# Sequence 1's tokens transposed on VectorE from rows folded in DRAM, two output copies issued two leaves later, and wf's first sums on GpSimd

## The chip, the cores and the metric

The kernel runs on one core of a Trainium2 chip. The metric is the device time of one execution in microseconds (us), as the median of several runs. The profile names the engines PE (TensorE, matmuls), PEld (its weight loads), DVE (VectorE), ACT (ScalarE), POOL (GpSimd) and SP (SyncE, which here only issues DMAs). Each engine takes its own instructions strictly in the order in which they stand in its queue; an instruction that waits for a semaphore holds up everything behind it on that engine, DMA issues included.

## The reference

Four sequences of 512 tokens, 512 features, in float32. One layer: a gated linear scan, then a feed-forward part with a Hadamard transform, each between layer norms and with a residual.

```python
x = x + layernorm(attn(layernorm(x)))
x = x + layernorm(ffn(layernorm(x)))

def attn(h):                       # Wi, Wf, Wg, Wo: 512 x 512
    i, f, g = h @ Wi.T, h @ Wf.T, h @ Wg.T
    gate = sigmoid(f);  v = silu(i) * (1 - gate)
    o_t = gate_t * o_(t-1) + v_t            # scan over the tokens
    o = o * rsqrt(mean(o * o) + eps) * gnorm_w * g * sigmoid(g)
    return o @ Wo.T

def ffn(h):                        # W1, W3: 2048 x 512, W2: 512 x 2048
    return fwht(silu(h @ W1.T) * (h @ W3.T)) @ W2.T
```

## The kernel before

**Products in seven pieces.** Every large matrix product is done by a seven-product scheme on 2x2 blocks (Strassen-Winograd). `ORDER` gives the products as P1, P2, P6, P5, P7, P3, P4; each reads one block or sum of blocks of the weights (A11 to A22, S1, S2, S3, S4) and one of the tokens (B11 to B22, T1 to T4). `combine_left` makes S1 and S2 (step 0) and S3 and S4 (step 1); `combine_right` makes T1 to T4. P1 and P2 read raw blocks alone; P6, the third, needs S2 and T2. The three PSUM banks of a product are X (P1, P6, P7, P4), Y (P2) and Z (P5, P3). A bank gathers: P4, say, is added into the bank that P7 left, so it waits until P7's value has been read out. P1, P6, P5 and P4 are read out by a copy on ACT, P2, P7 and P3 by an addition on DVE (L537).

**Units.** `attn_unit(b, u)` does one piece of the scan part of sequence b: u = 0 and u = 1 are the two halves of Wi and Wf (and end in the gate and the scan), u = 2 is Wg. The order begins with units (0,0), (0,1), (0,2), (1,0), (1,1). `run` walks through the seven products of a unit. After product k it takes what `beside[k]` lists, and, after every product if the unit is `dense`, else after products 1, 3, 5 and 6, one entry of the list `fill` (other work for PE: output products, the quarters of the Hadamard transform of W2). `seven` also takes entries of `acts` and `sums` at fixed products: activations and DVE or POOL work that belongs to earlier products.

**Order on the engines.** PE and SP have the order in which the code is written. The others are scheduled when the kernel is built; `behind(what)` puts work behind a named earlier instruction, and `tc.high_priority` moves it forward. What results is a fixed order for each engine.

**Layer norm and transposing.** `normalize_tiles(b, "a", i0, n)` takes statistics of a token tile (128 tokens) on DVE (`st_a`, L289; `mv_a`, L290), the inverse root as a power on POOL (`rs_a`, L264), the bias on DVE (`nb_a`, L303), and applies both on ACT (`xn_a`, L318). For sequence 0 the four tiles are done one by one as x arrives. The normalized tokens must be transposed, and there are two ways:

- `transposes(b, name)`: on PE against the identity, two groups of eight (`pt_a`, L439), copied from PSUM to `xt_a` by DVE and ACT (L446, L444), then `combine_right`. Sequences listed in `ON_TENSOR` go this way: 0 and 1.
- for the others, `normalize_tiles` writes the normalized tiles to DRAM in two DMAs from POOL's queue (`xnd_a`, L327, 512 KB each), `load_fold` reads them back folded (`fold_a`; from SP, with the 32-row blocks of four feature groups beside each other on the partitions), and `transpose_fold` transposes 32x32 blocks on DVE (L497), eight instructions, and then calls `combine_right`.

**Weights.** Raw weights of sequence 0's units come from the inputs (`wi`, `wf`, `wg`; two DMAs of 256 KB each, L199) and are combined on DVE; with S1 to S4 beside them they are 896 KB and are written to DRAM by POOL's queue (`s_wi`, `s_wf`, `s_wg`, L179). Later sequences load that from SP (L186). The `stream` pool has five buffers, so a load also waits until an earlier unit has let one go. The first unit's S1 and S2 are made by `combine_weights(2, (0,))`, S3 and S4 later.

**The end of sequences 0 and 1.** `OutputNorm.half_onto` normalizes the feed-forward output `f` (POOL root, ACT L412) and adds it to the residual rows, kept in DRAM, by an accumulating DMA from POOL's queue (`s_x<-f`, L416); the next DMA on the same queue copies those rows to the output (`out_dram<-s_x`, L417), and waits for the first. POOL also has work of the running products in its queue there (`q`, L946, part of the outer combination in `ffn_pair`).

Of the kernel before, what the change touches and what calls it, by code (L numbers as in the profile page):

```python
# [44 lines left out]
def kernel(  # L45
# [14 lines left out]
    nc = tc.nc  # L60
# [5 lines left out]
    NJ = NF // 2  # L66
# [3 lines left out]
    URGENT, SOON = 400, 200  # L70
# [23 lines left out]
    fill = deque()  # L94
# [7 lines left out]
    beside = {}  # L102
# [52 lines left out]
    def combine_left(t, eng, steps=(0, 1)):  # L155

        if 0 in steps:
            eng.tensor_add(t[:, S1], t[:, A21], t[:, A22])  # L158
            eng.tensor_sub(t[:, S2], t[:, S1], t[:, A11])
        if 1 not in steps:  # L160
            return
        eng.tensor_sub(t[:, S3], t[:, A11], t[:, A21])
        return eng.tensor_sub(t[:, S4], t[:, A12], t[:, S2])  # L163
# [41 lines left out]

    uncombined = []

    def combine_weights(n=None, steps=(0, 1)):
        for _ in range(len(uncombined) if n is None else n):
            key, t = uncombined.pop(0)  # L210
            read["combined"] = combine_left(t, nc.vector, steps)
            if 1 in steps:
                kept(key, t)
            else:
                uncombined.append((key, t))
# [3 lines left out]
    def load_attn_w(b, u):  # L219
        if u < 2:  # L220
            attn_w[b, u] = weight(wi, "wi", u, b), weight(wf, "wf", u, b)
        else:
            attn_w[b, u] = weight(wg, "wg", 0, b), weight(wg, "wg", 1, b)
# [26 lines left out]
    def behind(what):  # L250


        return tc.issue_after(read[what].ins)
# [12 lines left out]

    xns, xnd = {}, {}

    ON_TENSOR = ("a", 0), ("a", 1)

    def normalize_tiles(b, name, i0, n, later=False):

# [78 lines left out]
    class OutputNorm:  # L351
# [47 lines left out]
        def half_onto(self, i, rows, to):  # L399

            b, mv = self.b, self.mv[:, 2 * i : 2 * i + 2]
            name = f"{self.name}_{b}_{i}"
            for t in range(2):
                nc.vector.bn_aggr(mv[:, t, :], self.st[:, 2 * i + t])
            r = inverse_root(mv, self.eps, name)
            nm = small.tile([P, 2], F32, tag="nb", name=f"nm_{name}", bufs=8)
            nc.vector.tensor_scalar(nm, mv[:, :, 0], -1.0, None, ALU.mult)
            nc.gpsimd.tensor_mul(nm, nm, r)

            def piece(t):  # L410
                y_t = self.y[:, i, t, :]
                nc.scalar.activation(  # L412
                    y_t, y_t, AF.Identity, bias=nm[:, t : t + 1], scale=r[:, t : t + 1]
                )
                if t:
                    nc.gpsimd.dma_start(out=rows, in_=self.y[:, i], accum_op=ALU.add)  # L416
                    nc.gpsimd.dma_start(out=to, in_=rows)  # L417

            scaled.extend([1, partial(piece, t)] for t in range(2))

# [700 lines left out]
    def load_w2(pieces):  # L1121
        for j in pieces:
            if j in (4, 5):
                t = stream2.tile([P, 3, D], F32, tag="w", name=f"w2p_{j}")
            else:
                t = work.tile([P, 3, D], F32, tag="ht", name=f"w2p_{j}", bufs=4)
            if j >= HALVES:
                for b, r in enumerate((chunks(j).start, chunks(j).start + 2)):
                    nc.sync.dma_start(
                        out=t[ts(b, P // 2), 0:2, :], in_=w2_quarters[:, r, :, :]  # L1130
                    )
            else:
                rows = w2_rows[:, chunks(j), :]
                for k in ((0, 1), (1, 2)) if j == 0 else ((0, 2),):
                    nc.sync.dma_start(
                        out=t[:, k[0] : k[1], :], in_=rows[:, k[0] : k[1], :]
                    )
            w2_p.append(t)
# [140 lines left out]
    later = uncombined[2:]  # L1279
    del uncombined[2:]  # L1280
    with behind("xt"):
        combine_weights(2, (0,))
    with behind("power"):
        load_constants()

# [12 lines left out]
        butterfly_b(0)  # L1298
    for k, j in ((0, 2), (1, 3)):
        low_step(k, "P2", butterfly_u, j)  # L1300
    fill.extend([None] + quarters[:2])
    attn_unit(0, 1)
    with behind("P3"):
        with tc.high_priority(offset=URGENT):
            combine_weights(2)
        with tc.high_priority(offset=SOON):
            apply = [normalize_tiles(1, "a", i, 2, True) for i in (0, 2)]
    load_attn_w(1, 0)
    load_w2(range(4, NJ))

    def behind_copy(*makes):
        with behind("copy"):
            for make in makes:
                make()

    fill.extend(
        [None, partial(behind_copy, *apply)] + transposes(1, "a")
    )
    for k, c in ((0, 0), (2, 1)):
        beside.setdefault(k, []).append(  # L1320
            partial(behind_copy, partial(scale_wo, wo_t[0], c))
        )
    attn_unit(0, 2)
    load_attn_w(1, 1)
    load_x(2)

    def beside_copies(b, places):
# [2 lines left out]
            late = [normalize_tiles(b, "a", i, 2, True) for i in (0, 2)]  # L1330
        for t, place in enumerate(places):
            yield place, partial(behind_copy, partial(late[t // 2], range(t % 2, t % 2 + 1)))

    def transpose_beside(b, name, places=((1, "P2"), (4, "P7"), (6, "P3"))):


        def step(make, what):
            with behind(what), tc.high_priority(offset=SOON):
                make()

        for make, (k, what) in zip(transpose_fold(b, name), places):
            beside.setdefault(k, []).append(partial(step, make, what))

    fill.extend([None] * 3 + attn_out(0) + quarters[-4:])
    for k, what, make, at in (
# [291 lines left out]
```

## Time and profile before

| | |
|---|---|
| median of 3 runs | 783.71 us (783.34 to 784.11) |
| profiled execution, its own time | 784.42 us |
| span of the profile | 782.6 us |
| PE busy | 764.2 us (98%) |
| DVE, ACT, POOL busy | 615.7, 240.0, 357.2 us |
| unit (0,0): P1, P6, P4 start | 11.32, 17.14, 24.72 us |
| units (0,1), (0,2), (1,0), (1,1) start | 26.55, 41.07, 55.06, 74.58 us |

Start times are from the timeline of PE, counted from the start of the span; 1.8 us of the execution lie outside the span. The granted TensorE clock is 1.00 in every stretch of 10 us up to 770. In the profile's lines a group reads: start, duration, engine, line, operation, output<-inputs, shapes, count, and in brackets the idle time ahead of it and what ended that. SPq and POOLq stand for the instructions that an engine issues without being counted as busy.

### The profile page before, as it was taken

What the parts mean: (1) busy time and instruction counts of PE and PEld (TensorE: products, weight loads), DVE (VectorE), ACT (ScalarE), POOL (GpSimd) and SP (SyncE); (2) the same over time, 40 slices, a digit from 0 to 9 for tenths busy, and PEclk for the clock granted to TensorE, in tenths of its full rate; (3) what the DMA queues carried; (4) which work ended last, traced back from release to release, by engine and by line L of the source; (5) the groups of instructions that cost most, each with busy time, mean ns of one, the idle gap of its engine ahead of it and who ended that gap; (6) DMA issues with size and microseconds to landing.
All of it is one profiled execution on the core that took longest, in us unless ns stands there. A gap on an engine that the chain in (4) does not pass through costs nothing.

```text
span 782.6 us, 10415 instructions
## 1 busy us (share of the span) xinstructions
PE 764.2 (98%) x3560; PEld 658.0 (84%) x3560; DVE 615.7 (79%) x1158; ACT 240.0 (31%) x337; POOL 357.2 (46%) x444
## 2 busy tenths in 40 slices
PE   8999999999999999999999999999999999999994
PEld 6788788887888888888888888888888888888883
DVE  5879989799877597898689799998645666664786
ACT  4383664545436232424112111021321100111112
POOL 1111202213302001177596968677767756664372
PEclk9999999999999999999999999999999999999998
DMA  9998474896899899983429420442456141121112
GB/s 267 394 339 313 155 263 168 253 342 227 295 368 336 269 295 397 361 269 99 157 80 217 149 78 9 150 99 70 99 173 159 52 151 55 54 75 74 54 55 107
DMA packets 90516, 147.29 MB, mean 188 GB/s; under 512 B 15136, under 2 KB 68512, under 8 KB 90208
## 3 DMA queue, kind: packets, MB, share of 16 engines
q1 hardware_dynamic: 79376, 94.98, 39.5%
q0 software_dynamic: 10368, 50.34, 17.6%
q10 hardware_dynamic: 720, 1.31, 0.5%
q8 instruction: 28, 0.46, 0.3%
q14 instruction: 24, 0.20, 0.1%
HBM read 97.32 MB, written 51.38 MB: 190 GB/s over the span
## 4 chain that ended last, share of the span: by engine, by line
PE 85%; DVE 7%; DMA 3%; POOL 2%; issue 2%; ACT 0%; SPq 0%; POOLq 0%; DVEq 0%; ACTq 0%
PE X_u L1042 18%; PE X_po L743 13%; PE X_a L562 9%; PE Z_u L1042 9%; PE Z_po L743 7%; PE X_f L562 5%; PE Z_a L562 4%; PE Y_u L1042 4%; PE Y_po L743 3%; PE X_y L670 3%; PE Y_a L562 2%; PE Z_f L562 2%; DMA wf<-in_Wf_dram 2%; PE Z_y L670 2%; POOL q L946 1%
## 5 line engine op out<-in xcount | busy, mean ns | idle before, releaser
L743 PE MATMUL X_po<-w,ht 128*128 128x256 f32 x512 | 139.1, 379 | 0.0
L1055 DVE TENSOR_TENSOR q<-X_u,q 128x512 f32<-128x512 f32 x132 | 90.5, 685 | 47.2 <-PE X_u L1042 42.7
L1042 PE MATMUL X_u<-xq,wl 128*128 128x256 f32 x480 | 123.3, 381 | 0.0
L743 PEld LDWEIGHTS X_po<-w,ht 128*128 128x128 f32 x512 | 97.3, 190 | 13.2
L1042 PEld LDWEIGHTS X_u<-xq,wl 128*128 128x128 f32 x480 | 90.5, 190 | 14.8 <-DVE q L1055 1.7
L987 ACT ACTIVATE q<-q 128x1024 f32<-128x1024 f32 x24 | 25.4, 1058 | 163.1 <-DVE q L1055 86.8
L946 POOL TENSOR_TENSOR q<-q,q 128x512 f32<-128x512 f32 x48 | 62.7, 1322 | 22.7 <-DVE q L1055 21.3
L743 PE MATMUL Z_po<-w,ht 128*128 128x256 f32 x256 | 69.1, 379 | 1.2 <-ACT f L539 1.2
L1055 DVE TENSOR_TENSOR q<-Z_u,q 128x512 f32<-128x512 f32 x72 | 49.4, 686 | 18.5 <-PE Z_u L1042 18.2
L562 PE MATMUL X_f<-xt_f,w 128*128 128x256 f32 x256 | 60.4, 381 | 1.9 <-DVE d_f L537 1.5
L1042 PE MATMUL Z_u<-xq,wl 128*128 128x256 f32 x240 | 61.6, 379 | 0.0
L179 POOL DMA_DIRECT2D s_w<-w x24 | 13.1, 545 | 99.9 <-DVE w L163 70.3
L562 PEld LDWEIGHTS X_f<-xt_f,w 128*128 128x128 f32 x256 | 48.2, 190 | 9.6 <-DVE d_f L537 2.3
L1052 ACT COPY q<-X_u 128x512 f32<-128x512 f32 x36 | 21.0, 585 | 114.6 <-PE X_u L1042 114.6
L743 PEld LDWEIGHTS Z_po<-w,ht 128*128 128x128 f32 x256 | 48.6, 190 | 8.2 <-ACT f L539 1.6
L1042 PEld LDWEIGHTS Z_u<-xq,wl 128*128 128x128 f32 x240 | 45.6, 190 | 6.2
L1042 PE MATMUL X_u<-og,wl 128*128 128x256 f32 x192 | 49.6, 381 | 1.1 <-DVE q L1055 1.1
L1055 DVE TENSOR_TENSOR q<-Y_u,q 128x512 f32<-128x512 f32 x42 | 28.8, 686 | 24.0 <-PE Y_u L1042 19.5
L158 POOL TENSOR_TENSOR ht<-ht 128x256 f32<-128x256 f32 x24 | 20.2, 843 | 59.8 <-DVE ht L999 59.8
L537 DVE TENSOR_TENSOR f<-X_po,f 128x512 f32<-128x512 f32 x51 | 34.8, 683 | 15.3 <-PE X_po L743 14.4
L1042 PEld LDWEIGHTS X_u<-og,wl 128*128 128x128 f32 x192 | 36.1, 190 | 7.2 <-issue 1.2
L999 DVE TENSOR_TENSOR ht<-q 128x512 f32<-128x512 f32 x48 | 41.3, 874 | 0.0
(230 smaller groups left out, 1589.6 us busy)
## 6 DMA issues: line engine op xcount, KB each, us to landing
s_w<-w POOLq DMA_DIRECT2D x24, 896.0 KB, 5.9
wl<-s_w SPq DMA_DIRECT2D x168, 128.0 KB, 2.5
w<-s_w SPq DMA_DIRECT2D x22, 896.0 KB, 7.8
w<-in_W_dram SPq DMA_DIRECT2D x32, 256.0 KB, 6.8
wi<-s_wi SPq DMA_DIRECT2D x6, 896.0 KB, 9.3
wf<-s_wf SPq DMA_DIRECT2D x6, 896.0 KB, 8.1
wg<-s_wg SPq DMA_DIRECT2D x6, 896.0 KB, 6.3
w_h<-w2p POOLq DMA_DIRECT2D x8, 512.0 KB, 5.5
```

What stands on the lines that cost most here:

```text
L158: eng.tensor_add(t[:, S1], t[:, A21], t[:, A22])
L179: return nc.gpsimd.dma_start(out=saved[key], in_=t)
L537: read[what] = nc.vector.tensor_add(to, ps[which], to)
L562: nc.tensor.matmul(ps[:, n, :], w[:, a, c, :], xt[:, bb, c, :], start=first and n == 0 and c == 0, stop=c == 1, skip_group_check=True,)
L670: nc.tensor.matmul(ps[:, t, :], og[:, a, c, ts(t, P)], w[c][:, bb, :], start=first and t == 0 and c == 0, stop=c == 1, skip_group_check=True,)
L743: nc.tensor.matmul(ps[:, t, :], hts[b, m][:, a, ts(t, P)], w[m][:, W2[bb], :], start=first and k == 0, stop=m == ms[-1], skip_group_check= ...
L946: queued.append(make(*args).ins)
L987: nc.scalar.activation(q[k][:, 0], q[k][:, 0], AF.Silu)
L999: nc.vector.tensor_mul(t[:, h : h + 3 : 2], d[:, 0, n].rearrange("p (t f) -> p t f", t=2), d[:, 1, n].rearrange("p (t f) -> p t f", t=2),)
L1042: nc.tensor.matmul(ps[which][:, k, :], w[:, k, a, :], x[:, bb, :], start=first and k == 0, stop=True, skip_group_check=True,)
L1052: read["copy"] = nc.scalar.copy(y, ps[which])
L1055: last = nc.vector.tensor_add(y, ps[which], z)
```

## The change

1. `ON_TENSOR` holds sequence 0 alone. Sequence 1 goes the way of sequences 2 and 3: its statistics are placed behind P2 of unit (0,0), its four tiles are applied on ACT beside products 0 to 3 of unit (0,1), they are written to DRAM (2 x 512 KB), and `load_fold(1, "a")` reads them back in four DMAs of 256 KB. That call stands ahead of `load_attn_w(1, 0)`, so on SP's queue the four loads stand behind the loads of wo and ahead of wi and wf of sequence 1, of the eight loads of W2's other quarters, and of what follows. The DVE transposes are placed beside products 4, 5 and 6 of unit (0,2).
2. Unit (0,1) becomes dense, and `fill` gets entries of None so that the two quarters stand at the same products as before. In PE's queue the sixteen transposes of sequence 1 are gone, and nothing else moves.
3. S1 and S2 of the first wf tile are made on POOL, not DVE. In the order that results, POOL has: the roots of tiles 0, 1 and 2 of sequence 0, the two sums of wf, the root of tile 3, then the rest. DVE keeps the two sums of wi, now behind the bias of tile 3.
4. In `half_onto`, the copy to the output is no longer issued right behind the accumulating DMA but goes to the list `sums` behind two empty entries. In POOL's queue this changes one place: two additions of `q` stand between the last accumulating DMA and the first of the two copies, and one between the copies.

The rest of the order of DVE and ACT shifts by a few places up to unit (1,1). The core of the diff:

```diff
-    def combine_weights(n=None, steps=(0, 1)):
+    def combine_weights(n=None, steps=(0, 1), eng=None):
...
-            read["combined"] = combine_left(t, nc.vector, steps)
+            read["combined"] = combine_left(t, eng or nc.vector, steps)
...
-    ON_TENSOR = ("a", 0), ("a", 1)
+    ON_TENSOR = (("a", 0),)
...
                     nc.gpsimd.dma_start(out=rows, in_=self.y[:, i], accum_op=ALU.add)
-                    nc.gpsimd.dma_start(out=to, in_=rows)
+                    copy = partial(nc.gpsimd.dma_start, out=to, in_=rows)
+                    sums.extend([lambda: None, lambda: None, copy])
...
     with behind("xt"):
-        combine_weights(2, (0,))
+        combine_weights(1, (0,))
+        combine_weights(1, (0,), nc.gpsimd)
...
-    fill.extend([None] + quarters[:2])
-    attn_unit(0, 1)
-    with behind("P3"):
-        with tc.high_priority(offset=URGENT):
-            combine_weights(2)
-        with tc.high_priority(offset=SOON):
-            apply = [normalize_tiles(1, "a", i, 2, True) for i in (0, 2)]
-    load_attn_w(1, 0)
-    load_w2(range(4, NJ))
+    fill.extend([None] * 3 + quarters[:1] + [None] + quarters[1:2])
...
-    fill.extend(
-        [None, partial(behind_copy, *apply)] + transposes(1, "a")
-    )
+    with behind("P2"):
+        apply = [normalize_tiles(1, "a", i, 2, True) for i in (0, 2)]
+    for k, t in ((0, 0), (1, 1), (2, 2), (3, 3)):
+        beside.setdefault(k, []).append(
+            partial(behind_copy, partial(apply[t // 2], range(t % 2, t % 2 + 1)))
+        )
+    attn_unit(0, 1, True)
+    with behind("P3"):
+        with tc.high_priority(offset=URGENT):
+            combine_weights(2)
+    load_fold(1, "a")
+    load_attn_w(1, 0)
+    load_w2(range(4, NJ))
...
+    transpose_beside(1, "a", ((4, "P7"), (5, "P3"), (6, "P3")))
     attn_unit(0, 2)
```

`transpose_beside` is the helper that sequences 2 and 3 already use; its definition only moves up.

## The prediction

> **What bounds the kernel now.** I read the page's totals first, then the chain that ended last in order of time, then the timelines of single engines around the three edits. Every time is microseconds from the start of the span.
>
> ```profile
> span 782.6 us, 10415 instructions
> PE 764.2 (98%) x3560; PEld 658.0 (84%) x3560; DVE 615.7 (79%) x1158; ACT 240.0 (31%) x337; POOL 357.2 (46%) x444
> ```
>
> PE is busy for 98% of the span, so PE work that goes is gained only if PE does not wait for something new. The chain's first pieces:
>
> ```profile
> 6.22 7.68 DMA wf<-in_Wf_dram
> 13.92 7.68 DMA wf<-in_Wf_dram
> 24.72 3.72 PE X_a L562 x16
> ```
>
> The second half of wf lands at 13.90; from 24.72 on the chain is nearly all PE. What happens around 13.90 (timelines of POOL, DVE, ACT and PE; a bracket is the idle time ahead and its cause):
>
> ```profile
> 10.26 0.55 POOL L264 TENSOR_TENSOR rs_a<-rs_a,power 128x1 f32<-128x1 f32 x1 [1.28 <-DVE rs_a L261]
> 13.93 0.43 DVE L158 TENSOR_TENSOR wf<-wf 128x256 f32<-128x256 f32 x1 [2.21 <-DMA wf<-in_Wf_dram]
> 11.40 0.84 ACT L318 ACTIVATE xn_a<-x,nb_a,rs_a 128x512 f32<-128x512 f32 x1
> 14.16 0.65 ACT L444 COPY xt_a<-pt_a 128x256 f32<-128x256 f32 x2
> 13.25 1.11 PE L439 MATMUL pt_a<-ident,xn_a 128*128 128x128 f32 x8
> 17.14 1.13 PE L562 MATMUL X_a<-xt_a,wi 128*128 128x256 f32 x4 [1.05 <-DVE xt_a L169]
> ```
>
> The root of token tile 3 (L264) is done at 10.81, long before wf; the tile is normalized at 11.40, transposed at 13.25; P6 of the first unit starts at 17.14, after waiting 1.05 for T2. The transposes that the change removes, and PE's neighbours there:
>
> ```profile
> 51.43 1.11 PE L439 MATMUL pt_a<-ident,xn_a 128*128 128x128 f32 x8
> 52.38 1.89 PE L562 MATMUL X_a<-xt_a,wg 128*128 128x256 f32 x8
> 54.11 1.11 PE L439 MATMUL pt_a<-ident,xn_a 128*128 128x128 f32 x8
> 55.06 1.03 PE L562 MATMUL X_a<-xt_a,wi 128*128 128x256 f32 x4
> ```
>
> PE runs through here without a gap. Sequence 1's first unit starts at 55.06, its wf products at 55.92. Last, what the same fold loads cost where the kernel has them already (SP's queue; then KB each and median us to landing):
>
> ```profile
> 206.26 2.12 SPq L472 DMA_DIRECT2D fold_a<-xnd_a  x4
> 209.81 0.55 SPq L186 DMA_DIRECT2D wf<-s_wf  x1
> wf<-s_wf SPq DMA_DIRECT2D x1, 896.0 KB, 15.0
> 259.27 2.15 SPq L472 DMA_DIRECT2D fold_f<-xnd_f  x4
> 261.51 1.09 SPq L186 DMA_DIRECT2D w<-s_w  x2
> w<-s_w SPq DMA_DIRECT2D x2, 896.0 KB, 8.9
> ```
>
> From the first fold load to the landing of the second 896 KB weight behind it: 209.81 + 15.0 - 206.26 = 18.5 where POOL's queue wrote two 896 KB weights at the same time (209.20, 210.20), and about 262.1 + 8.9 - 259.27 = 11.7 where it did not.
>
> **Part 1, wf's first sums on POOL.** In the instruction order POOL now has: roots of tiles 0, 1 and 2, the two sums of wf, root of tile 3. POOL takes its queue in order, and the sums wait for the wf half that lands at 13.90. So tile 3's root, done at 10.81 before, waits: two sums of 0.84 (the page's row of POOL's 128x256 adds, 843 ns; the wl adds of that shape take 0.73) to 15.6, root 0.55 to 16.2, bias on DVE 0.16 to 16.4, tile normalized on ACT 0.81 to 17.2. Behind that instruction stand on ACT two w2p copies (1.10), P1's copy (0.57) and two xt copies (0.65): 19.5. DVE waits at the bias with wi's sums behind it (two, 0.34 apart; ready by 17.1), then T1 and T2, 0.68 each and 0.1 between: about 20.6 instead of 17.1. P6 starts 3.5 later. P5, P7 and P3 follow at 1.73 each; before, PE had 0.6 of waiting ahead of 24.72, because DVE stood at the next wf (landing 21.60) with P7's addition behind it; that slack goes. Cost: +2.9. The lower end has PE alone late: transposes done at about 18.1, P2 until 19.9, so 2.7 - 0.6 = +2.1. Below that it goes only if tile 3's root is not held; then this term is nothing, since the wf landing at 21.60 still sets 24.72.
>
> **Part 2, transposes.** PE loses two groups of eight; each takes 0.95 from its start to the next instruction's (51.43 to 52.38, 54.11 to 55.06): -1.9. The rest of PE's order is unchanged, the quarters' matmuls included. DVE loses six copies of about 0.35 and gains eight transposes of 0.33 (four took 1.33 at 152.20): +0.6 on DVE, paid while PE waits for weights.
>
> The Trainium skill's VectorE: DVE Perf Modes, Rules for kernel authors, says to transpose 128x128 on TensorE where a PSUM destination is acceptable, which speaks against this change; this trace's price for keeping it there is the 1.9 of PE.
>
> The new way is a chain: statistics on DVE, root on POOL, four normalized tiles on ACT, two POOL writes of 512 KB to DRAM, four SP loads of 256 KB, transposes. Its place: DVE resumes unit 0 with P7's addition at about 26.4. To the second bias stand about fifteen instructions at a pitch of 0.60 (w2p butterflies, products' additions), four statistics at 0.57, two of 1.14 and 0.7 of small ones: 14.3, so 40.7 less about 0.4 for what is spread behind it: 40.3. Two tiles on ACT at 0.8: 41.9; the second write is issued at 42.0 and lands 3.7 later (median of xnd_a around 88): 45.7. Only then may SP issue the fold.
>
> Behind the fold on SP stand wi and wf of sequence 1 (issued at 33.98 and 40.40 before), eight w2p loads, the next wi and wf, and x of sequence 2. So wf lands between 45.7 + 11.7 = 57.4 and 45.7 + 18.5 = 64.2. POOL's two s_wg writes (896 KB each) are issued at about 45 to 46 here, beside the fold, as in the longer row, but without that row's extra 512 KB write and with a small head start. I take 14.9, a little under the middle of 15.1: 60.6. PE would be at its wf products at 55.92 + 2.9 - 1.9 = 56.9: a wait of +3.7 (ends +0.5 and +7.3). The fold itself lands 8 to 10 after its issue by the rows at 206 to 216, by 55.7; transposes, T1, og and T2 take 5.1 more, 60.8, before P6 needs T2 at about 63.
>
> ACT's new tiles stand ahead of P5's copy in unit (0, 1), which then ends about 0.7 before P3 needs its bank, and DVE's P7 addition ends 0.4 before P4. I cost both at nothing: what PE would lose is taken out of the wait for wf, which is longer. Without that wait, each miss is up to 1. The later SP loads (3.9 MB to the next wf) need 10 at the 390 GB/s of windows 20 to 50, and the s_wo writes 4.7: 75.5, against 74.58 + 4.7 = 79.3 when unit (1, 1) starts. Covered.
>
> The Trainium skill's TensorE: Matmul & The Clock Gate, Part 1, says that PE's clock halves after an idle window of about 3.4 us. Here the granted clock falls to 0.50 about 5 us after the last matmul (772.3 to 777.3), and no gap before is that long. The new gaps of about 3.7 are near that rule; one cold window would add an estimated 1.7, which I leave out by the trace's 5.
>
> **Part 3, output copies later.** POOL stood still for its accumulating write:
>
> ```profile
> 592.15 0.74 POOL L417 DMA_DIRECT2D out_dram<-s_x  x1 [3.65 <-DMA s_x<-f]
> 603.99 0.70 PE L743 MATMUL Z_po<-w,ht 128*128 128x256 f32 x2 [1.23 <-ACT f L539]
> ```
>
> Behind it stood q additions; ACT's gate waited for the last of them, the copy of Z_po for the gate, PE for the copy. With two additions ahead of the copy POOL is done about 3.6 earlier, and PE's gap goes: 603.99 instead of 602.16 + 0.43, -1.4. If the additions wait for DVE anyway, it is 0. In the order this is the only place where POOL's instructions change.
>
> **Sum.** Against the profiled execution (784.42: span 782.6 and 1.8 around it): +2.9 - 1.9 + 3.7 - 1.4 = +3.3, 787.7. The median of the runs is 783.71, 0.7 lower: 787.0.
>
> **Rivals.** (1) Weights in time: SP's queue is idle while it waits, so nothing else is loading, and the 11.7 row holds. The wait is 0.5, the sum +0.1: 783.8, no change. For it: the emptied load queue; against it: the s_wg writes. (2) The other end, 18.5: wait 7.3, sum +6.9: 790.6. (3) Faster: tile 3's root is not held on POOL. Then part 1 is 0, and the whole chain to the fold, which hangs on P7, moves up by the same 2.9. With the weights at the 11.7 row the sum is -1.9 + 0.5 - 1.4 = -2.8: 780.9 (with 14.9 it would be +0.4). It decides at the landing of wf: if that comes before about 10.3, when the root's input is ready, the sums cost the root little. Against it stands 13.90 in this trace, with the same loads ahead of it. (4) The copies' move does nothing: 1.4 more than each case.
>
> **How the numbers follow.** The forecast, slower, has 0.55; the longer end 0.12; no change (with the low edge of the forecast) 0.18; faster 0.15. A difference under 0.2% (1.6 us) can't be told from none here. So slower 0.67, same 0.18, faster 0.15. The range of 782.6 to 790.5 leaves out about 0.1 on each side: below lies most of the faster case, above half of the longer end.
>
> **What would show it.** On POOL two wf additions at 13.9 and tile 3's root after 15.5; P6 of unit (0, 0) near 20.6. No L439 group after 20. SP's fold near 46 and wi after it; in sequence 1's first unit a PE wait for wi or wf of 2 to 5, its start near 59. No gap on PE near 603. I am wrong if PE enters sequence 1 before 55, or if the root of tile 3 stays near 10.3.

## The result, and the profile after

The changed kernel takes 792.63 us (median of 4 runs, 789.72 to 795.74) against 783.76 (783.34 to 784.11) for the kernel before on the same chip. The ratio of the means is 1.0114, 95% interval 1.0067 to 1.0161: slower, by more than the forecast (787.0) and beyond the range's upper end (790.5). The profiled execution took 790.59; before's took 784.42, so the two traces differ by +6.17, and those 6.17 can be followed through the trace.

The page's totals after:

```profile
span 788.8 us, 10385 instructions
PE 765.8 (97%) x3544; PEld 658.6 (83%) x3544; DVE 617.6 (78%) x1158; ACT 241.6 (31%) x335; POOL 360.1 (46%) x448
```

PE has 16 instructions fewer, as the change says, and yet 1.6 us more busy time. The same matmuls took longer, so part of the loss is not waiting but clock: two windows of 3.41, told of below, ran at a granted clock of 0.50. Each keeps PE busy for about 1.7 longer; against the two stand the transposes' 1.9, which are gone.

**The start, timelines of POOL, ACT and PE** (line numbers are those of the changed kernel, which lie one higher from L417 on):

```profile
12.64 0.73 POOL L158 TENSOR_TENSOR wf<-wf 128x256 f32<-128x256 f32 x1 [3.82 <-DMA wf<-in_Wf_dram]
14.12 0.55 POOL L264 TENSOR_TENSOR rs_a<-rs_a,power 128x1 f32<-128x1 f32 x1
14.90 0.81 ACT L318 ACTIVATE xn_a<-x,nb_a,rs_a 128x512 f32<-128x512 f32 x1 [3.53 <-DVE nb_a L303]
15.77 1.03 PE L440 MATMUL pt_a<-ident,xn_a 128*128 128x128 f32 x4 [2.59 <-ACT xn_a L318]
16.59 1.92 PE L563 MATMUL Y_a<-xt_a,wi 128*128 128x256 f32 x4
19.75 1.03 PE L563 MATMUL X_a<-xt_a,wi 128*128 128x256 f32 x4
```

POOL waits 3.82 for wf, and tile 3's root comes out of it at 14.67 instead of 10.81: it is held, as the prediction said. The tile is normalized at 14.90 instead of 11.40, and PE stands 2.59 ahead of the last four transposes. Behind that gap the granted clock is 0.50 from 16.06 to 19.47, and P2's two groups take 3.16 (16.59 to 19.75), where before they took 1.73. When PE enters unit (0,1) it is 1.83 late (28.38 against 26.55).

**Unit (0,1), timelines of PE, PEld and DVE after, then the lines of before that answer to them:**

```profile
34.43 1.03 PE L563 MATMUL Z_a<-xt_a,wf 128*128 128x256 f32 x4
38.17 2.62 PE L1161 MATMUL h<-w2p,had 64*64 64x512 f32 x8 [2.72 <-DVE w2p L1151]
40.72 2.07 PE L563 MATMUL X_a<-xt_a,wi 128*128 128x256 f32 x4
39.35 0.20 PEld L1161 LDWEIGHTS h<-w2p,had 64*64 64x64 f32 x6 [1.02 <-DVE w2p L1152]
37.36 0.66 DVE L1151 TENSOR_TENSOR w2p<-w2p 128x512 f32<-128x512 f32 x1
38.61 0.69 DVE L1152 TENSOR_TENSOR w2p<-w2p 128x512 f32<-128x512 f32 x1
```

```profile
33.55 1.09 PE L1160 MATMUL h<-w2p,had 64*64 64x512 f32 x8
25.25 0.68 DVE L1150 TENSOR_TENSOR w2p<-w2p 128x512 f32<-128x512 f32 x1
27.05 0.68 DVE L1151 TENSOR_TENSOR w2p<-w2p 128x512 f32<-128x512 f32 x1
```

This is the step that the prediction did not have. The group h is one quarter of W2's Hadamard transform; its two inputs are made by `butterfly_u` on DVE. Before, DVE had finished them 7.6 and 5.8 ahead of PE. After, they come 12 later, at 37.36 and 38.61. The description of the change says that DVE's order shifts by a few places; these two stand 21 places later. Ten of the instructions now ahead of them are sequence 1's statistics and what belongs to them, the other eleven are work that stood behind the butterflies before. PE waits 2.72 for the first, its weight loads wait 1.02 more in the middle of the group, and the four matmuls behind it take 2.07 instead of 1.03. The windows tell why the last of these is so (columns: window, length, busy time of PE, PEld, DVE, ACT and POOL, granted clock, DMA share, GB/s):

```profile
36.54:39.94 3.40, 1.63 (x8) 0.39 (x8) 2.78 (x8) 2.67 (x3) 2.23 (x3) 1.00 1.03 389
39.95:43.36 3.41, 3.41 (x12) 2.19 (x7) 0.73 (x2) 3.24 (x4) 1.09 (x2) 0.50 0.54 207
```

After a window in which PE was busy for 1.63 of 3.41, the granted clock is 0.50 for the next. PE is then busy all through, at half speed, and loses 3.41/2 = 1.7. Altogether 2.72 + 1.02 + 1.7 = 5.4, and with the 1.83 from the start and a rest of 0.2 PE is 7.4 late (43.84 against 36.40).

**The fold and sequence 1's weights, SP's queue and PE:**

```profile
46.12 1.93 SPq L473 DMA_DIRECT2D fold_a<-xnd_a  x4
60.60 1.03 PE L563 MATMUL X_a<-xt_a,wi 128*128 128x256 f32 x4
61.59 1.13 PE L563 MATMUL X_a<-xt_a,wf 128*128 128x256 f32 x4
64.91 1.10 PE L563 MATMUL X_a<-xt_a,wi 128*128 128x256 f32 x4 [0.46 <-DVE xt_a L169]
```

Unit (1,0) starts at 60.60 instead of 55.06: +5.54, the 7.4 less the 1.9 of the two groups of transposes. wf lands at 61.55, and PE starts on it at 61.59, +5.67 against 55.92. There is hardly a wait left to see, because PE is late already. P6 then waits 0.46 for T2, which stands on DVE behind the new transposes, and starts at 64.91, +6.11 against 58.80.

**The output copies, timelines of PE and DVE after, and DVE before:**

```profile
597.87 1.13 PE L1043 MATMUL Z_u<-og,wl 128*128 128x256 f32 x4 [1.55 <-DVE q L1056]
594.55 2.67 DVE L1000 TENSOR_TENSOR ht<-q 128x512 f32<-128x512 f32 x1
```

```profile
588.89 0.68 DVE L999 TENSOR_TENSOR ht<-q 128x512 f32<-128x512 f32 x1
```

PE's gap ahead of Z_po is gone, but a new one of 1.55 stands 12 earlier in PE's order, behind a DVE product that takes 2.67 where before it took 0.68. Nothing is gained there.

### The profile page after: what moved, and what is told of

Its sections match the earlier page's. It is cut to its first block, busy times and chain, and to the rows that moved or that the text cites. A ratio compares the mean times of both kernels' runs of the same rounds, so it can differ in the third digit from the quotient of the medians.

```text
span 788.8 us, 10385 instructions
## 1 busy us (share of the span) xinstructions
PE 765.8 (97%) x3544; PEld 658.6 (83%) x3544; DVE 617.6 (78%) x1158; ACT 241.6 (31%) x335; POOL 360.1 (46%) x448
## 4 chain that ended last, share of the span: by engine, by line
PE 85%; DVE 9%; DMA 2%; issue 1%; POOL 1%; SPq 1%; ACT 0%; POOLq 0%; DVEq 0%; ACTq 0%
PE X_u L1043 18%; PE X_po L744 13%; PE X_a L563 9%; PE Z_u L1043 9%; PE Z_po L744 7%; PE X_f L563 5%; PE Z_a L563 4%; PE Y_u L1043 4%; PE Y_po L744 3%; PE X_y L671 3%; PE Y_a L563 2%; PE Z_f L563 2%; PE Z_y L671 2%; PE Y_f L563 1%; DMA w<-in_W_dram 1%
## 5 line engine op out<-in xcount | busy, mean ns | idle before, releaser
L1056 DVE TENSOR_TENSOR q<-Z_u,q 128x512 f32<-128x512 f32 x72 | 49.4, 687 | 18.1 <-PE Z_u L1043 17.8
L1043 PE MATMUL Z_u<-xq,wl 128*128 128x256 f32 x240 | 61.6, 379 | 0.0
L538 DVE TENSOR_TENSOR f<-X_po,f 128x512 f32<-128x512 f32 x51 | 34.9, 684 | 15.0 <-PE X_po L744 14.9
L1000 DVE TENSOR_TENSOR ht<-q 128x512 f32<-128x512 f32 x48 | 43.8, 926 | 0.0
```

What stands on the lines that cost most here:

```text
L538: read[what] = nc.vector.tensor_add(to, ps[which], to)
L1000: nc.vector.tensor_mul(t[:, h : h + 3 : 2], d[:, 0, n].rearrange("p (t f) -> p t f", t=2), d[:, 1, n].rearrange("p (t f) -> p t f", t=2),)
L1043: nc.tensor.matmul(ps[which][:, k, :], w[:, k, a, :], x[:, bb, :], start=first and k == 0, stop=True, skip_group_check=True,)
L1056: last = nc.vector.tensor_add(y, ps[which], z)
```

## Experiments

The ratios compare means with those of the kernel before on the same chip. "Before" and "after" name the base of each edit.

**Part 1 alone** (before, with wf's sums on POOL).

```diff
-        combine_weights(2, (0,))
+        combine_weights(1, (0,))
+        combine_weights(1, (0,), nc.gpsimd)
```

> The kernel before with the first part alone: the second half-sum pair of wf on POOL. POOL's order is then two wf sums ahead of the root of token tile 3. By the prediction P6 of the first unit starts about 20.6 and the time rises by 2.1 to 2.9, to 785.9 to 786.6. By the reading of the changed kernel P6 is at about 19.8 (wf landed earlier there) and a part of the loss is a lower granted clock behind the idle time; at 24.72 about 1.9 of it are left: 785.6. A rival: without the fold's work on DVE behind it the loss is taken up again before unit (0, 1), and the time does not change.

Measured: 786.49 (785.15 to 788.63, 6 runs), ratio 1.0033 [1.0021, 1.0046], so +2.6. The root is held and the size is the term's. In its trace PE waits 2.7 at the transposes, the clock is 0.50 for the window behind that wait (16.73 to 20.14), P6 of unit (0,0) starts at 19.94 (+2.80), and unit (1,0) at 57.19, which is +2.13, the lower end. (That execution took 788.04, since it has the second loss told of below.)

**The change without part 1.**

```diff
-        combine_weights(1, (0,))
-        combine_weights(1, (0,), nc.gpsimd)
+        combine_weights(2, (0,))
```

> The changed kernel with wf's first sums back on DVE, so that tile 3's root is not held; the fold and the later copies stay. By the prediction's terms: -2.9 for part 1, 785 or less with the wait for wf at 3.7 unchanged. By the reading of the trace: P6 at 17.1, unit (0, 1) at 26.5 as before, but the quarter h of w2p still waits about 2.5 to 3 for DVE's butterflies (L1150), which stand behind the sequence-1 statistics on DVE, and the granted clock falls behind that gap: a loss of 4 to 5 by unit (1, 0), less the 1.9 of the transposes. Time 787 to 789.

Measured: 793.69 (789.39 to 796.06, 6 runs), ratio 1.0112 [1.0088, 1.0136]: as slow as the whole change. Its PE:

```profile
36.64 3.16 PE L1161 MATMUL h<-w2p,had 64*64 64x512 f32 x8 [3.01 <-DVE w2p L1151]
62.29 1.13 PE L563 MATMUL X_a<-xt_a,wf 128*128 128x256 f32 x4 [2.36 <-DMA wf<-s_wf]
```

PE now comes to the quarter 1.8 earlier (33.63 against 35.45) and waits 3.01; it enters unit (1,0) at 58.90 (+3.84) and then waits 2.36 for wf, after which it is +6.37 late. Two barriers stand one behind the other: what is saved ahead of the first is waited for at the second. Which of them would cost what alone is what the next runs ask.

**The first barrier alone** (before, and only statistics, roots and normalized tiles of sequence 1 moved into unit (0,1); PE and SP have the order of before, the transposes stay on PE). The core of the edit, the rest being the list entries that keep PE's order:

```diff
-        with tc.high_priority(offset=SOON):
-            apply = [normalize_tiles(1, "a", i, 2, True) for i in (0, 2)]
...
+    with behind("P2"):
+        apply = [normalize_tiles(1, "a", i, 2, True) for i in (0, 2)]
+    for k, t in ((0, 0), (1, 1), (2, 2), (3, 3)):
+        beside.setdefault(k, []).append(
+            partial(behind_copy, partial(apply[t // 2], range(t % 2, t % 2 + 1)))
+        )
```

> The kernel before with one thing of the change alone: sequence 1's statistics, roots and four normalized tiles moved up into unit (0, 1), where the changed kernel has them. The transposes stay on PE, nothing is folded, wf's sums stay on DVE, the copies stay. PE's and SP's instruction orders are those of before, DVE's has the statistics ahead of the butterflies of w2p 2 and 3. By the prediction's steps, which cost this displacement at nothing: 783.9. By the reading of the trace: h in unit (0, 1) waits 2.5 to 3 for DVE's butterfly (L1151 or L1150) and PE then runs at half clock for some 3 to 5 us, so unit (1, 0) starts 5 to 6 late and nothing gives it back: 788.5 to 790. Between the two: if only the wait counts, about 787.

Measured: 789.82 (789.32 to 790.99, 5 runs), ratio 1.0073 [1.0061, 1.0085]. There is no fold, no later weight load and no root held on POOL in this kernel, and it loses 5 to 6 us. Its PE and PEld:

```profile
35.88 3.16 PE L1160 MATMUL h<-w2p,had 64*64 64x512 f32 x8 [3.00 <-DVE w2p L1150]
37.06 0.29 PEld L1160 LDWEIGHTS h<-w2p,had 64*64 64x64 f32 x6 [1.02 <-DVE w2p L1151]
38.97 1.76 PE L562 MATMUL X_a<-xt_a,wi 128*128 128x256 f32 x4
```

The wait of 3.0, the 1.0 inside the group and 1.7 of half clock make 5.7. PE had come 0.67 earlier to this place (32.88 against 33.55), and it is 5.03 late behind it and stays so.

**How much of that is clock** (the kernel just told, and twenty matmuls of the identity into the quarter's own PSUM bank ahead of it; they are overwritten).

```diff
+        if j == HALVES:
+            for _ in range(20):
+                nc.tensor.matmul(ps[0][:, 0:P], ident, ident, start=True, stop=True)
```

> The kernel with the statistics alone moved up (its profiled execution took 789.3, h waited 3.0 for DVE, and the granted clock was 0.50 for 3.4 after it), with 20 matmuls of the identity put on PE ahead of h, into the bank that h then overwrites. They fill the 3.0 in which PE waits, and are done before DVE is. If the half clock is drawn by PE's idle time, h starts as late as there, the clock stays at 1.00, and 3.4/2 = 1.7 comes back: 787.6 to 788.2. If the clock falls for another reason, or only the wait counts, the time is 789.3 to 790.

Measured: 788.58 (787.16 to 793.46, 7 runs), ratio 1.0069 [1.0045, 1.0093]. The medians differ too little beside their spread to show it; the traces do: 787.38 against 789.32. Windows around the place, without the filling and with it:

```profile
33.45:36.86 3.41, 0.98 (x2) 0.19 (x2) 3.41 (x9) 2.00 (x3) 2.19 (x3) 1.00 1.11 345
36.87:40.28 3.41, 3.27 (x10) 1.43 (x10) 0.90 (x3) 2.46 (x4) 0.72 (x1) 0.50 1.05 411
```

```profile
32.00:35.41 3.41, 3.41 (x29) 3.31 (x29) 3.41 (x8) 1.52 (x3) 0.82 (x2) 1.00 1.10 330
35.42:38.83 3.41, 3.41 (x28) 2.43 (x28) 2.33 (x6) 1.49 (x3) 2.09 (x2) 1.00 1.09 403
```

DVE's butterfly starts at 35.06 in both. With PE kept busy the clock stays at 1.00, and PE is 3.69 late instead of 5.03, though the filling itself outlasted DVE by about 0.25. So some 1.3 to 1.6 of the loss is the half clock.

**Butterflies first** (after, the late quarter's butterflies written ahead of the unit).

```diff
+        butterfly_u(2)
...
-    for k, j in ((0, 2), (1, 3)):
+    for k, j in ((1, 3),):
```

> The changed kernel with the two butterfly additions of w2p tile 2 (which PE's quarter h waits for) queued on DVE ahead of the sequence-1 statistics, as their place was before; everything else as changed. By the prediction's steps this moves nothing on PE, since the displacement on DVE was costed at nothing: the time of the changed kernel. By the reading of the trace: PE's wait of 2.7 ahead of h and the half clock behind it go, so PE reaches sequence 1's first unit at about 57 instead of 60.6. There two answers: if wf's landing at about 60.5 to 62 is then the later, PE waits there 3 to 4 for wf and the gain is 1 or less (the recorded wait of 3.7 then appears); if the weights are in time, the gain is 4 to 5, 786 to 787 in the state of the profiled execution.

Measured: 800.27 (798.49 to 802.91, 5 runs), ratio 1.0205 [1.0187, 1.0222]. The expectation missed. The wait at h is gone, but the scheduler moved the statistics behind, and the four tiles came out as one block on ACT:

```profile
39.91 5.02 ACT L318 ACTIVATE xn_a<-x,nb_a,rs_a 128x512 f32<-128x512 f32 x4 [1.95 <-DVE nb_a L303]
64.07 2.05 PE L563 MATMUL X_a<-xt_a,wi 128*128 128x256 f32 x4 [4.56 <-DVE xt_a L498]
```

The fold was issued at 48.48, and PE waited 4.56 for the transposes. This edit moved the disturbance; it did not remove it.

**Statistics early instead** (after without part 1; the statistics at once behind wf's last sums, so that neither they nor the butterflies are late), and the **same order without the fold** (transposes on PE, copies as before).

```diff
-    with behind("P2"):
+    with behind("combined"), tc.high_priority(offset=URGENT):
         apply = [normalize_tiles(1, "a", i, 2, True) for i in (0, 2)]
```

> The changed kernel without part 1, and with the statistics of sequence 1 queued on DVE with the highest priority right behind the last sums of wf, so that they stand ahead of the butterflies of the pair but those of w2p 2 come in time again; the fold then goes out earlier, at about 38 to 41 instead of 44.9. If the h wait and the clock behind it are what costs, h starts within 1 of 33.6. Then the wait for wf of sequence 1 is what is left: by the 17.4 from the fold's issue to wf's landing in the kernel without part 1 (44.85 to 62.3), wf lands at 56 to 58 and PE, at wf at 54, waits 2 to 4: 783 to 786, about the time before. If the weights come in time as well, PE enters unit (1, 0) 1.9 earlier and the time is 781.5 to 782.5.

> The kernel with the statistics queued early (796.4), without the fold: sequence 1 is transposed on PE again and the output copies are where they were before. What is left of the change is the statistics' place, now ahead of the butterflies but in time for h. If the fold's queueing ahead of the weights on SP is what cost that kernel its 12, this one is at 783.5 to 785 and unit (1, 0) starts at 55.1, as before. If the early statistics cost as well (P4's or h's wait, ACT), it is 786 or more.

Measured: with the fold 796.38 (792.91 to 798.03, 5 runs), ratio 1.0139 [1.0116, 1.0162]; without it 783.67 (783.42 to 785.61, 12 runs), ratio 1.000 [0.9991, 1.001]. The kernel without the fold differs from that of the first barrier in this one line, the statistics' place, and loses nothing where the other loses 5 to 6: it is DVE's order that costs there, and not the work. The fold's way costs 11 to 12 all told (11 by the ratio, 12.2 by the medians on its chip), without any wait at h. PE of the kernel with the fold:

```profile
57.54 2.05 PE L563 MATMUL X_a<-xt_a,wi 128*128 128x256 f32 x4 [3.26 <-DMA wi<-s_wi]
61.66 2.07 PE L563 MATMUL X_a<-xt_a,wf 128*128 128x256 f32 x4 [2.08 <-DMA wf<-s_wf]
```

This is the second barrier by itself: 3.26 + 2.08, and half clock from 57.51 for three windows. PE is 8.48 late behind it, 12.8 at the end, with another wait of 4.4 near 200 (below). The fold was issued at 42.53 here, 3.6 earlier than in the changed kernel, and wf landed at 61.62 against 61.55. So the landing did not follow the fold's issue.

**What sets that landing.** POOL writes s_wg, 2 x 896 KB, in the same stretch. First the weights were put ahead of the fold on SP (and the transposes ahead of `og` on DVE):

```diff
-    load_fold(1, "a")
     load_attn_w(1, 0)
+    load_fold(1, "a")
```

> The kernel with the statistics early, the fold kept, but wi and wf of sequence 1 queued on SP ahead of the four fold loads, and unit (0, 2)'s gating products on DVE held behind the eight transposes. Then PE should not wait for wi or wf (3.3 and 2.1 there). The fold goes out at about 41, behind wf's buffer, and lands by 50; the transposes can start at about 53. If the weights' place was the cost, PE enters unit (1, 0) at 53.2 to 54.5 instead of 55.06: 781.9 to 783.5, faster than before. If the fold then comes late instead, PE waits for the transposes at the start of unit (1, 0), by 2 or more, with the half clock behind it: 786 or more.

Measured: 792.12 (789.75 to 794.72, 6 runs), ratio 1.0099 [1.0075, 1.0122]. PE still waits 4.0 at unit (1,0), now because the fold lands at 57.43, 13.4 after its issue. A next kernel was to hold s_wg's writes back by the program order alone:

> The kernel with the weights ahead of the fold (792.1; PE waited 4.0 for the fold, which was issued at 44.1 and landed at 57.4), with one more edit: POOL's two s_wg writes of 896 KB, which went out at 43.2 and 44.2 into the same transfers, are held until product P7 of unit (0, 2), about 50. If the shared transfers are what delays the fold, some 4.7 MB between 41 and 57 become 2.9 MB, the fold lands at about 51 to 52, PE enters unit (1, 0) at 53.2 to 54.5 without a lower clock, and the time is 782 to 784 (up to 787 if the later wait X_f near 190 is then of the longer kind). If the fold's small pieces are slow by themselves, it lands at 55 or later and the time is 788 or more.

Measured: 794.91 (791.43 to 795.57, 5 runs), ratio 1.0131 [1.0106, 1.0157]. The edit did not do what it was to do: the writes went out at 43.71 and 44.71 all the same, so it only repeats the kernel ahead of it. With a real dependence on POOL (a 128x1 addition that reads the scan of unit (0,1)) the writes wait; with the weights first, and then with the fold first as in the change:

```diff
+        junk = small.tile([P, 1], F32, tag="junk", name="junk")
+        last = os_[0][:, 1, 1, T - 1 : T]
+        read["junk"] = nc.gpsimd.tensor_tensor(junk, last, last, ALU.add)
+        with behind("junk"):
+            for make in held:
+                make()
```

> Statistics early, weights ahead of the fold on SP, and POOL's two s_wg writes (896 KB each) held behind a 128x1 addition on POOL that reads the scan of unit (0, 1), so until about 52. Without them the fold, issued at 44.1, landed at 57.4 and 58.7. If the transfers of the stretch as a whole set its landing, 1.8 MB less of 4.7 MB bring it to 51 to 53, PE enters unit (1, 0) at 53.3 to 54.5, and the time is 782 to 784. If the fold's own pieces (512 bytes) set it, it lands at 56 or later, PE waits 3 or more, and the time is 788 or more.

> Statistics early, fold ahead of the weights as in the change, and the two s_wg writes held in the same way until about 52. Without the hold wf of sequence 1 landed at 61.6 and PE waited 3.3 for wi and 2.1 for wf. If the transfers as a whole set it, wf lands at 56 to 58, PE waits 1 to 3 in all, and the time is 783 to 787. If the order fold, wi, wf on SP's queue sets it alone, wf stays at 60 to 62, the time at 792 or more.

Measured: weights first 788.04 (784.51 to 790.25, 12 runs), ratio 1.005 [1.0033, 1.0067], the fold landing at 54.38; fold first 786.61 (783.58 to 789.84, 12 runs), ratio 1.0036 [1.0018, 1.0053]. In the second, POOL and PE:

```profile
52.43 1.13 POOL L179 DMA_DIRECT2D s_wg<-wg  x2 [0.32 <-issue]
53.20 1.03 PE L565 MATMUL X_a<-xt_a,wi 128*128 128x256 f32 x4
55.90 1.13 PE L565 MATMUL X_a<-xt_a,wf 128*128 128x256 f32 x4 [1.68 <-DMA wf<-s_wf]
```

wf lands at 55.86, 14.3 after the fold's issue; with s_wg beside it, it took 19.1 (the kernel with early statistics). Between the fold's issue and wf's landing the queues moved 303 GB/s for 19.09 there and 274 GB/s for 14.30 here, so 5.8 and 3.9 MB, and the DMA engines were busy all through (share 1.01 and 1.03): the difference is the 1.8 MB of s_wg. PE enters unit (1,0) at 53.20, 1.86 earlier than before: the two groups of transposes, to 0.04. Then 1.68 of it goes into the wait for wf.

**The changed kernel again, and the second loss.** The changed kernel's runs differ by 6 us, before's by 0.8. It was run again on another chip.

> The changed kernel itself once more. Its four times so far are 789.7, 790.6, 794.7 and 795.7, its one profile is of the shorter kind. Reading: the 5 between the two kinds is one more wait of PE with the half clock behind it, at PE's wait X_f <- DVE d_f near 195, which was 1.5 in the shorter kind and 4.6 in the kernel with the butterflies first, where DVE waited 3.0 for a load of w at 184.6. If the profiled execution here is of the longer kind, that place has a PE wait of 3 or more; if it is somewhere else, this reading is wrong.

Measured: 799.43 (792.83 to 802.39, 5 runs; a sixth took 805.17 and is not counted in the ratio), ratio 1.0178 [1.0145, 1.0211]. PE, DVE and two windows of its profiled execution (796.36), then PE of before:

```profile
199.65 3.78 PE L563 MATMUL X_f<-xt_f,w 128*128 128x256 f32 x8 [3.65 <-DVE d_f L538]
178.69 0.43 DVE L158 TENSOR_TENSOR w<-w 128x256 f32<-128x256 f32 x1 [2.06 <-DMA w<-in_W_dram]
194.63:198.04 3.41, 1.37 (x13) 0.71 (x11) 3.04 (x7) 2.17 (x3) 1.59 (x3) 1.00 0.25 101
198.05:201.46 3.41, 1.81 (x4) 1.52 (x5) 3.41 (x9) 1.56 (x3) 0.73 (x1) 0.50 0.85 320
```

```profile
190.02 1.99 PE L562 MATMUL X_f<-xt_f,w 128*128 128x256 f32 x8 [1.50 <-DVE d_f L537]
```

In before PE waits 1.50 at this place (at 190.02), and the clock stays. Here DVE first stood 2.06 for a raw weight, PE waits 3.65, and the clock is halved for two windows. Unit (1,0) had started 6.8 late; behind this place it is near 12. In the changed kernel's first profile the wait was 1.50, as in before, and the loss stayed at 6.2. The same two waits go together in seven traces, part 1 alone among them: what PE waits beyond 1.50 is what DVE stood for the raw weight, to 0.1 (2.15 and 2.06 here, 3.08 and 3.00 with the butterflies first, 0.95 and 0.86 with part 1 alone).

SP loads x of sequence 3 in that stretch, between the raw weights. In the kernel with s_wg held (fold first) and in before, that load was put behind them:

```diff
+        if (b, m) == (0, 0):
+            load_x(3)
...
-    load_x(3)
```

> Statistics early, fold first, s_wg held, and x of sequence 3 queued behind w's loads on SP in unit (2, 2). If the w load's landing makes the spread, the times lie together (within 2) and near the best of the kernel without this edit, 783 to 784.5; PE's wait X_f near 190 is 1.5. If the spread comes from elsewhere, it stays at 783.5 to 790. With the wait of 1.7 for wf still there, no more than 0.5 below the time before is expected.

> The kernel before with this one edit, x of sequence 3 queued behind w's loads. Its wait X_f is 1.5, set by what DVE has queued and not by the load, which lands 2.3 before DVE asks for it. So no change: 783.4 to 784.4. If X_f's 1.5 hangs on the load after all, it gains up to 1.5.

Measured: 784.23 (783.31 to 788.45, 12 runs), ratio 1.001 [0.9992, 1.0028]; and on before's base 783.64 (782.79 to 784.1, 11 runs), ratio 0.9992 [0.9977, 1.0007]. So even with both losses made small, and 1.5 of waiting for wf left in its trace, the change's fold is no faster than the kernel before. The spread shrank (8 of 12 runs lie within 783.3 to 784.7, the others at 786.2 to 788.5) and did not go. Before has such runs too: 4 of its 23 on this chip took 786.5 to 789.0, the others 783.0 to 784.7. No trace of those four was kept.

**Part 3 alone**, with two empty entries ahead of the copy as in the change, and with one.

```diff
-                    nc.gpsimd.dma_start(out=to, in_=rows)
+                    copy = partial(nc.gpsimd.dma_start, out=to, in_=rows)
+                    sums.extend([lambda: None, lambda: None, copy])
```

> The kernel before with the third part of the change alone: the output copies queued two additions later. By the prediction's sum PE's gap of 1.23 at 603.99 goes and nothing takes its place: -1.4, 782.3. By the reading of the changed kernel's trace the gap goes too, but the q additions of POOL, now without the pause, run beside DVE's additions of two SBUF operands and hold one of them up (2.67 instead of 0.68): PE waits 1 to 2 for q's products a few us earlier, and the time is 783.5 to 784.3, no change. If DVE's long addition does not appear here, the second reading is wrong.

> The kernel before with the output copies queued one addition later instead of two. With two, PE's gap of 1.2 at 604 went, and one of 1.54 came at 591.55, because DVE's addition (L1000) took 2.66 instead of 0.68 beside two POOL additions. If POOL's additions beside it are the cause, one of them there stretches it by about half, 1.0: PE's gap at 591.5 is 0.5 or none, POOL reaches the second copy about 1.5 earlier than before, and the time is 0.3 to 1 below before: 783 to 783.6. If the long addition has another cause, it takes 0.68 or 2.66 here and the time is that of before or of the kernel with two.

Measured: 783.9 (783.5 to 784.98, 11 runs), ratio 1.000 [0.9992, 1.0009]; with one entry 784.07 (783.48 to 784.69, 12 runs), ratio 0.9999 [0.9988, 1.001]. In its trace POOL has the same order as with two entries, two additions of q ahead of the first copy, and DVE's product takes the same 2.66; so this run repeats the other, and a single addition was not tested. POOL, DVE and PE of the first:

```profile
587.26 3.08 POOL L947 TENSOR_TENSOR q<-q,q 128x512 f32<-128x512 f32 x2
587.64 0.68 DVE L538 TENSOR_TENSOR f<-Y_po,f 128x512 f32<-128x512 f32 x1
588.24 2.66 DVE L1000 TENSOR_TENSOR ht<-q 128x512 f32<-128x512 f32 x1
591.55 1.13 PE L1043 MATMUL Z_u<-og,wl 128*128 128x256 f32 x4 [1.54 <-DVE q L1056]
```

POOL's additions now run where POOL stood still before. DVE's product of two SBUF operands falls beside them and takes 2.66 (0.68 at 588.89 in before); its addition from PSUM, beside the same POOL additions, takes its 0.68. The next product, at 592.21, takes 1.86. DVE's read-out of Z_u comes late (590.82, 589.49 before), and PE waits 1.54 for it: what the copies' move freed is lost at another place.

## Why the prediction was wrong

Two steps failed. In the mechanism it is the displaced work on DVE, put at nothing. In the number it is mostly part 3, counted as a gain, and a loss near 190 that no term had.

**Part 1** held: the root held on POOL, 2.1 to 2.9 foreseen. Alone it costs 2.1 in the trace up to unit (1,0) and 2.6 by the runs; in the changed kernel's trace it is 1.83. That the size fits is in part luck. wf landed at 12.6 and not at 13.90, so the transposes were done by 16.6 and not at 18.1; but P2 ran at half clock, which the sum did not have, and ended at 19.75 against the 19.9 foreseen.

**"I cost both at nothing."** This is the step of the mechanism that failed. It named ACT's tiles and DVE's P7 addition as the displaced work and looked at P3 and P4. It did not look at the butterflies, which stand in the same stretch of DVE's order and which PE's next quarter reads. Their cover before was 7.6 and 5.8, and in the new order they come 12 later. Alone this costs 5.0 in the trace and 0.73% [0.61, 0.85] in the runs. The order of DVE in the changed kernel shows it; the prediction took from that order only where the statistics stand, not what they push back. Its fifteen instructions ahead of the second bias include w2p butterflies; it counted their time and did not ask who reads them. Its reason, that what PE loses there is taken out of the wait for wf, came out all the same, by luck of size: the 5.4, the 1.83 and the −1.9 bring PE to the wf products 0.1 before they could start.

**The clock "by the trace's 5"** failed with it. The 5 was measured from the last matmul to the falling of the clock, and it was read as a length of idle time that is needed. The windows show something else: the clock changes on a grid of 3.41, and a window with PE busy for 1.63 of it was enough, with a gap of 2.72. The 5 in before fits that grid: the window 770.51 to 773.92, with PE busy for 1.79, kept the clock, the next one was idle, and the clock fell behind it. On that grid, from 12 to 215 in seven of the traces, the clock falls eight times, each time behind a window with PE busy for 1.63 or less; 1.85, 1.89 and 1.90 kept it at 1.00. The busy time alone does not decide near half a window: in the kernel with the weights ahead of the fold, a window with 1.53 (52.53 to 55.94) was followed by 1.00. The Trainium skill's TensorE: Matmul & The Clock Gate, Part 1, gives a free-running window of 3413 ns, which the grid of these traces confirms, and one idle window as the condition, which is stricter than what they show: less than half busy was enough in all eight falls.

**Transposes, −1.9**, held: 7.4 to 5.54 across them in the changed kernel, 1.86 where nothing else is late.

**The wait for wf, +3.7.** The place was right, and 60.6 for the landing was 0.95 short of the 61.55 measured: the fold went out 0.4 later, and the landing took 15.4 from there, not 14.9 (17.4 and 19.1 in the two kernels with an earlier fold, so that 14.9 came near is partly luck). The wait itself shrank to nearly nothing, because PE, predicted at 56.9, came at 61.4 through the missed step. So in this sum the two barriers do not add: the first alone gives +5.0, and the second holds PE to about the same time, or later, if the first is removed. That is why the profiled execution, at +6.17, is nearer to the sum's +3.3 than the missed 5.4 would make it: of the 2.9 between them 1.4 is part 3, 0.95 is the landing, and 0.4 lies between the wf products and P6, most of it the wait for T2, which the prediction held covered. That the landing hung on POOL's s_wg writes was said, as a reason for the longer row. What was not seen is that it hangs on them so far that an earlier fold gains nothing.

**Part 3, −1.4**, is 0, and in the profiled execution this is the largest part of the miss. The text allowed for 0 "if the additions wait for DVE"; what happened is the reverse: DVE waits beside POOL's additions. The Trainium skill's SBUF — State Buffer, Who interferes with whom, states it: a DVE instruction with two SBUF inputs contends with a GpSimd instruction that reads SBUF. Here it is 2.66 against 0.68, and the addition from PSUM is untouched.

**The second loss**, near 190 to 205, was in no term and no rival. By the repeated run's trace it is what separates the profiled +6.17 from the median's +8.9; the long runs of the first four left no trace of their own. PE's wait there is 1.5 in some executions and 2.2 to 4.6 in others, and the longer ones bring half clock. Shown is that DVE then waits for a raw weight from SP. Why that load comes late in some executions and not in others is not settled, nor whether before's own long runs have the same cause: moving x behind it narrows the spread, and four of 12 runs stay high.

The rivals: the short wait (783.8) and the faster case (780.9) are out; the copies' rival (+1.4 on each case) is right. The long wait's 790.6 is the profiled time almost exactly, but by chance: its 18.5 was 15.4, and it counts part 3 as a gain.

## What to carry to other kernels

When work is inserted on an engine, list every instruction that slides behind it in the new order and look up who reads each; the costly one here was not the inserted work's own chain but an unrelated butterfly whose reader stood next on PE. Where a stretch has two barriers in series, test each alone, and count bytes in the stretch before counting issue times: holding 1.8 MB of writes moved a weight's landing from 61.6 to 55.9, issuing the fold ahead of it 3.6 earlier moved it by nothing. A short PE gap can cost more than its length: 2.7 of waiting brought 1.7 of half clock.

## What the runs showed of the hardware

- The granted clock changes on a grid of 3.41 only: in every trace with more than one change the changes lie whole multiples of 3.41 apart. Before every fall from 10 on to 0.50 PE was busy for 1.63 or less of a window, and every window at 1.00 with 1.79 or more kept 1.00. In between it went both ways: 1.63 and 1.48 brought 0.50, 1.53 (weights ahead of the fold, 52.53) and 1.43 (part 1 alone, 774.48) kept 1.00. At 0.50, windows with 1.80 to 2.67 busy kept it there (as twice behind 57.51 in the kernel with early statistics); near 2.9 it went both ways, 2.94 kept it (butterflies first, 63.97) and 2.87 brought 1.00 back (early statistics, 200.87).
- A DVE product of two SBUF operands took up to 2.67 beside POOL's additions, four times its 0.68; a DVE addition from PSUM beside the same additions took its 0.68.
- Where a stretch is full of transfers, a load's landing followed the bytes in the stretch: wf, issued behind a fold at 42.53, 44.85 and 46.12 in three kernels, landed at 61.62, 62.25 and 61.55, with the DMA engines' share at 0.96 to 1.01 in between; with 1.8 MB of writes held, issued behind a fold at 41.56, it landed at 55.86.
